# An attention and mixture-of-experts layer on one core: a hand-ordered opening, units loaded a head ahead, and a mixture stage in program order with norms and routing in pieces

## The chip, the core and the metric

The kernel runs on one core of one Trainium2 chip. The core has five engines that run their own instruction streams: TensorE (PE in the profile, with PEld for its weight loads), VectorE (DVE), ScalarE (ACT), GpSimd (POOL) and SyncE (SP), which here issues the DMAs. Matrix products go to PSUM, everything else lies in SBUF. The metric is device microseconds of one execution; lower is better.

## What is computed

One layer over 4 sequences of 512 tokens with 256 features. Each sequence has six vectors of modulation, made from a small condition `c`. The tokens are normalised and modulated, go through causal attention with 16 heads of 128, and are added back under a gate; then they are normalised and modulated again, go through a mixture of eight expert networks of different widths (plus one shared network and a "core" branch), and are added back under a second gate.

```python
mod = (silu(c) @ wmod).reshape(4, 6, 1, 256)
sa, ca, ga, sb, cb, gb = (mod[:, i] for i in range(6))
ga, gb = (sign(g) * maximum(abs(g), 0.25) for g in (ga, gb))
h = layernorm(x) * (1 + ca) + sa
# attention: 16 heads, causal
k, q, v = (einsum('ihd,bpd->biph', W, h) for W in (W_K, W_Q, W_V))
attn = softmax(masked(q @ k.T) / sqrt(128))
x = x + ga * einsum('df,bqf->bqd', W_O, flat(attn @ v))
h = layernorm(x) * (1 + cb) + sb
# mixture: each token's two best experts by softmax(h @ router_w + router_b - cost)
d = h @ down_w + down_b
out = sum over k in (0, 1) of gate_k * sum over e of (
    gelu(gelu(d * mask_ke) @ w1_e + b1_e) @ w2_e + b2_e)
out = out + 0.1 * (gelu(gelu(d) @ shared_w1 + shared_b1) @ shared_w2 + shared_b2)
x = x + gb * (out @ up_w + up_b + gelu(h) @ core_w + core_b)
```

## The kernel before

**Numbers in two parts.** Most products are made of three: a value `a` is kept as `hi` (its rounding to the type fp32r) and `lo` (the rest, `rest()`, line 148), and `mm3` multiplies lo by hi, hi by lo and hi by hi (lines 140 to 142). So nearly every matrix that PE reads first needs a cast, mostly on ScalarE, and a subtraction, on VectorE or GpSimd. Weights are loaded as "units" of 128 x 512 numbers into a `stage` tile (two buffers) and parted into `wu` tiles (`load_unit`, line 185).

**Opening.** `x0` (the first sequence) in two pieces, `c`, the matrix `wmod`, and the first units are loaded on SP's queue. sc = silu(c) is made by an Exp on ScalarE and three operations on VectorE. `normed` makes mean and variance (`bn_stats`, `bn_aggr`), rstd on GpSimd, and xn. `modulation` (line 301) makes the shift and scale of a norm from sc and wmod; `modulated` (line 378) transposes xn on PE, applies them and parts the result into hTh and hTl. `make_gates` (line 319) makes the gates ga and gb for all four sequences as rows of four partitions, with VectorE at lines 333 to 338, and stores them; `gate_rows` reads them back, spread over the partitions.

**Attention.** 64 heads in the order of `order`: four groups of four heads, in each group all four sequences b. For each head `n`: q and k (`project`), the values (`values`, tile pv, half of a pair of heads at a time), the scores of four tiles of 128 queries with maxima on VectorE (L488), Exp on ScalarE (L498), reciprocals (L502) and the scaling of `e` on GpSimd (L503, called `by_sum`). `turned` transposes e in blocks of 32 on VectorE, writes them out (`moved`) and reads them back as aT, so that blocks come to their places. `parted` casts aT on ScalarE (L535) and makes its rest on GpSimd (L148). `mixed` multiplies by the values (pz) and makes zh and zl; `project_out` multiplies by W_O (po), and after the last head of a group adds the gated result to x. `LAG = 3`: a head's aT is used three heads later. `finish` starts the second norm, its modulation and the routing of a sequence once its last head is done.

**Mixture.** `before_chunks` makes pd = h @ down_w, its Gelu on ScalarE and its two parts ghh and ghl on VectorE. `Mixture` goes through 20 chunks of 128 hidden features (`ORDER` has the experts) and the shared network: `first` makes ph, its Gelu (hid), and where it is needed the parts ah (ScalarE) and al (VectorE); `second`, three chunks later (`FFN_LAG`), multiplies by w2 into acc. `expert` turns acc into a part of the sum on VectorE (L859), which GpSimd adds to oacc (L863). `gelu_inputs` makes gelu(h) for the core branch on GpSimd and ScalarE; `core` multiplies it; `outputs` multiplies by up_w, applies the gate and stores y. `route` makes the two best experts and their gates with about thirty small operations on VectorE, over 32 partitions, with two or three Exp or Tanh on ScalarE, and stores them; each expert's row is read back as `spread`.

**Order.** PE's order is the program's (`manual_schedule`). The other engines' order in this version is set by a planner, which orders by a simulated time; only the first norm's VectorE and ScalarE work is in program order. `issue_after(i)` puts what follows behind instruction i in the planner's order. `later[n]` has work to be emitted beside head n.

Of the kernel before, what the change touches and what calls it, by code (L numbers as in the profile page):

```python
# [11 lines left out]
F32 = mybir.dt.float32  # L12
# [6 lines left out]
P = 128  # L19
# [4 lines left out]
HG = 4  # L24
# [71 lines left out]
FFN_CORE = (19, 20)  # L96
BEFORE3 = 4
EARLY = 2


TO_PART = tuple(u for u, (_, in_parts) in UNITS.items() if in_parts)
PART_AT = (18, 20, 22, 24, 26, 28, 34, 36, 38, 40, 42)
# [11 lines left out]
def adaln_attention_moe_kernel(  # L114
# [51 lines left out]

    load_x(0, 2)
    cT = const.tile([P, DC, B], F32, tag="cT", name="cT")
    nc.sync.dma_start(cT, c_t.rearrange("(c p) b -> p c b", p=P))
# [15 lines left out]
    def load_unit(src, nm: str, early: bool = False):  # L185

        st = work.tile([P, 512], F32, tag="stage", name=f"st_{nm}")
        nc.sync.dma_start(st, src)
        u = const.tile([P, 2, 512], F32R, tag="wu", name=nm, bufs=10)
        hi, lo = u[:, 0], u[:, 1]  # L190
        if early:
            nc.scalar.copy(hi, st)
        else:
            nc.gpsimd.tensor_scalar(hi, st, 1.0, 1.0, ALU.mult, ALU.mult)
        rest(nc.gpsimd, lo, st, hi)
        return hi, lo
# [62 lines left out]
    sc_e = small.tile([P, DC, B], F32, bufs=1, tag="silu_e", name="sc_e")  # L259
    exp_c = nc.scalar.activation(sc_e, cT, AF.Exp, scale=-1.0)  # L260
    nc.vector.tensor_scalar(sc_e, sc_e, 1.0, None, ALU.add)
    nc.vector.reciprocal(sc_e, sc_e)
    sc = small.tile([P, DC, B], F32, bufs=1, tag="silu", name="sc")
    nc.vector.tensor_mul(sc, cT, sc_e)

    ct = const.tile([P, C_END], F32, tag="cols", name="cols")
    nc.gpsimd.dma_start(ct, cols)
    b1 = ct[:, C_B1:C_B2]
    with tc.issue_after(exp_c.ins):
        nc.scalar.activation(gb1, b1[:, :NCH], AF.Gelu)  # L270
    load_wm(0)
    wqk_u[0] = load_unit(wqk[0], "wqk0", True)
    wv_u[0] = load_unit(wv[0], "wv0", True)
    load_wm(1)
    load_wm(2)
    wqk_u[1] = load_unit(wqk[1], "wqk1", True)
    for b in range(1, B):
        load_x(b)
# [3 lines left out]
    nc.vector.memset(router_w, 0.0)  # L282
    nc.sync.dma_start(router_w[:, :, :E], router.rearrange("p (c n) -> p c n", n=E))
# [8 lines left out]
    nc.vector.memset(mask[:, : NT - 1, :], 0.0)  # L292
    make_causal_mask(nc, mask[:, NT - 1, :], mask_val=MASKED)
    maskf = mask.rearrange("p t k -> p (t k)")
    def mod_w(c: int, f: int, n: int) -> bass.AP:
        return wm[f // 512, c][:, f % 512 : f % 512 + n]
# [4 lines left out]
    def modulation(which: int):  # L301
        pt = psum.tile([P, 4, B], F32, tag="pj", name=f"pt_mod_{which}", bufs=3)
        for i in range(4):
            for c in range(DC):
                nc.tensor.matmul(
                    pt[:, i, :],
                    lhsT=mod_w(c, 3 * D * which + i * P, P),
# [3 lines left out]
                )  # L311
        m = modT[:, 4 * which : 4 * which + 4, :]
        nc.vector.tensor_copy(m[:, :2, :], pt[:, :2, :])
        nc.vector.tensor_scalar(m[:, 2:, :], pt[:, 2:, :], 1.0, None, ALU.add)


    gates_d = dram.tile([B, 2, D], F32, tag="gates", name="gates_d")

    def make_gates():
        pm = psum.tile([B, 2, D], F32, tag="pj", name="pm", bufs=3)  # L320
        for i in range(2):
            for c in range(DC):
                nc.tensor.matmul(
                    pm[:, i, :],
                    lhsT=sc[:, c, :],
                    rhs=mod_w(c, (3 * i + 2) * D, D),
                    start=(c == 0),
                    stop=(c == DC - 1),
                )
        g = work.tile([B, 2, D], F32, tag="kh", name="g_raw")  # L330
        nc.scalar.copy(g, pm)
        sgn = work.tile([B, 2, D], F32, tag="kl", name="g_sgn")
        nc.vector.tensor_scalar(sgn, g, 0.0, 2.0, ALU.is_ge, ALU.mult)
        mag = work.tile([B, 2, D], F32, tag="tmp", name="g_mag")
        nc.vector.tensor_scalar(mag, g, -1.0, None, ALU.mult)
        nc.vector.scalar_tensor_tensor(mag, mag, 0.25, g, op0=ALU.max, op1=ALU.max)
        gates = work.tile([B, 2, D], F32, tag="tmp", name="gates")
        nc.vector.scalar_tensor_tensor(gates, sgn, 1.0, mag, op0=ALU.subtract, op1=ALU.mult)
        nc.sync.dma_start(gates_d, gates)
# [8 lines left out]
    def normed(b: int, which: int):  # L348
# [3 lines left out]
        for t in range(NT):  # L352
            nc.vector.bn_stats(st[:, t, :], xs[b][:, t, :])
        for t in range(NT):
            nc.vector.bn_aggr(mv[:, t, :], st[:, t, :])
# [3 lines left out]
        xn = work.tile([P, DC, NT, P], F32, tag="xn", name=f"xn_{b}_{which}", bufs=1)  # L359
# [9 lines left out]
        return xn  # L369
# [8 lines left out]
    def modulated(b: int, which: int):  # L378
# [6 lines left out]
        first = not (b or which)  # L385
        whole = []
        for c in range(DC):
            ptr = psum.tile([P, S], F32, tag="pj", name=f"ptn_{b}_{which}_{c}", bufs=3)
            for t in range(NT):
                nc.tensor.transpose(ptr[:, ts(t, P)], xn[:, c, t, :], ident)  # L390
            scale = modT[:, 4 * which + 2 + c, b : b + 1]
            shift = modT[:, 4 * which + c, b : b + 1]

            if c and not first:
# [3 lines left out]
            whole.append(ptr)  # L398

            for d in (c,) if not first else range(DC) if c == DC - 1 else ():  # L400
                nc.scalar.copy(hi[:, d, :], whole[d])
# [798 lines left out]
```

## Time and profile before

| what | value |
|---|---|
| median of three runs | 810.0 us (808.84 to 810.09) |
| the profiled execution | 809.29 us |
| its span, first to last instruction | 807.5 us |
| mean granted clock of TensorE | 0.986 |
| first matmul / first value product pv | 6.95 / 18.11 us from the span's start |
| stage of attention with heads of all kinds | to about 618 us |
| mixture | from there to the end |

The span is what the profile shows; about 1.8 us of the execution lie around it. Engine times are busy times, so an engine can be nearly always busy and still not be the reason that the kernel lasts: what counts is which engine the others wait for. PE's ends are modelled; the distance between starts of successive matmuls is the surer measure of its pace. The granted clock is TensorE's alone: where it is under 1, part of the stretch ran at half clock.

### The profile page before, as it was taken

What the parts mean: (1) busy time and instruction counts of PE and PEld (TensorE: products, weight loads), DVE (VectorE), ACT (ScalarE), POOL (GpSimd) and SP (SyncE); (2) the same over time, 40 slices, a digit from 0 to 9 for tenths busy, and PEclk for the clock granted to TensorE, in tenths of its full rate; (3) what the DMA queues carried; (4) which work ended last, traced back from release to release, by engine and by line L of the source; (5) the groups of instructions that cost most, each with busy time, mean ns of one, the idle gap of its engine ahead of it and who ended that gap; (6) DMA issues with size and microseconds to landing.
All of it is one profiled execution on the core that took longest, in us unless ns stands there. A gap on an engine that the chain in (4) does not pass through costs nothing. (4 is left out here: it accounts for less than half of the span.)

```text
span 807.5 us, 14122 instructions
## 1 busy us (share of the span) xinstructions
PE 775.5 (96%) x4487; PEld 671.9 (83%) x4487; DVE 594.7 (74%) x1734; ACT 490.9 (61%) x1184; POOL 521.7 (65%) x523
## 2 busy tenths in 40 slices
PE   6889999999999999999999999999997999989997
PEld 5669998999999999999999999998896866767775
DVE  5968788777777667676777677778898486785665
ACT  3556667666666655666666656666656333656663
POOL 4745566896767579786758886566546155655675
PEclk9999999999999999999999999999998899999999
DMA  7465354665666667675556765545575332312221
GB/s 236 112 190 152 111 156 128 184 180 160 199 192 182 182 204 220 174 213 177 177 175 186 191 178 151 162 137 160 147 227 156 106 124 86 105 53 77 55 86 58
DMA packets 73218, 124.12 MB, mean 154 GB/s; under 512 B 8996, under 2 KB 51252, under 8 KB 73144
## 3 DMA queue, kind: packets, MB, share of 16 engines
q1 hardware_dynamic: 73112, 123.21, 52.3%
q8 instruction: 36, 0.59, 0.3%
q14 instruction: 38, 0.31, 0.1%
q0 software_dynamic: 32, 0.02, 0.0%
HBM read 73.05 MB, written 50.14 MB: 153 GB/s over the span
## 5 line engine op out<-in xcount | busy, mean ns | idle before, releaser
L148 POOL TENSOR_TENSOR aT<-aT,aTh 128x1152 fp32r<-128x1152 f32 x64 | 172.0, 2687 | 115.5 <-ACT aTh L535 115.4
L503 POOL TENSOR_SCALAR e<-e,inv 128x128 f32<-128x128 f32 (+3 forms) x256 | 135.7, 543 | 69.3 <-DVE inv L502 67.2
L498 ACT ACTIVATE e<-e,nmax 128x128 f32<-128x128 f32 (+3 forms) x256 | 143.9, 564 | 45.4 <-DVE nmax L488 44.5
L535 ACT CAST aTh<-aT 128x1152 fp32r<-128x1152 f32 x64 | 74.2, 1159 | 134.8 <-DMA aT<-moved 81.3
L488 DVE CUSTOM_DVE_ANT_0 e<-ps,mask 128x128 f32<-128x128 f32 (+3 forms) x256 | 120.1, 478 | 23.8 <-PE ps L482 14.6
L518 DVE STREAM_TRANSPOSE T<-e 128x384 f32<-128x384 f32 (+2 forms) x256 | 100.3, 445 | 7.8 <-POOL e L503 7.8
L148 DVE TENSOR_TENSOR zl<-pz,zh 128x512 fp32r<-128x512 f32 x64 | 44.0, 688 | 52.8 <-ACT zh L553 52.7
L140 PE MATMUL ps<-kh,ql 128*128 128x256 f32 (+2 forms) x192 | 71.2, 371 | 6.3 <-DVE nmax L488 6.2
L140 PE MATMUL po<-wo,zl 128*128 128x256 f32 x256 | 73.1, 285 | 0.6 <-DVE zl L148 0.6
L141 PE MATMUL po<-wo,zh 128*128 128x256 f32 x256 | 72.0, 281 | 0.0
L142 PE MATMUL po<-wo,zh 128*128 128x256 f32 x256 | 72.0, 281 | 0.0
L140 PE MATMUL pv<-wv,hTl 128*128 128x256 f32 x256 | 71.8, 281 | 0.0
L141 PE MATMUL pv<-wv,hTh 128*128 128x256 f32 x256 | 71.6, 280 | 0.0
L142 PE MATMUL pv<-wv,hTh 128*128 128x256 f32 x256 | 71.5, 279 | 0.0
L863 POOL TENSOR_TENSOR oacc<-oacc,part 128x512 f32<-128x512 f32 x28 | 40.9, 1462 | 43.5 <-DVE part L859 36.8
L502 DVE RECIPROCAL inv<-tot 128x1 f32<-128x1 f32 x256 | 40.2, 158 | 37.2 <-ACT e L498 29.6
L141 PE MATMUL ps<-kl,qh 128*128 128x256 f32 (+2 forms) x192 | 65.5, 341 | 0.2
L140 PE MATMUL pz<-aTh,vl 128*128 128x512 f32 (+2 forms) x192 | 65.5, 341 | 0.0
L141 PE MATMUL pz<-aT,vh 128*128 128x512 f32 (+2 forms) x192 | 65.4, 341 | 0.0
L142 PE MATMUL pz<-aTh,vh 128*128 128x512 f32 (+2 forms) x192 | 65.4, 340 | 0.0
L142 PE MATMUL ps<-kh,qh 128*128 128x256 f32 (+2 forms) x192 | 65.0, 339 | 0.0
L592 POOL TENSOR_TENSOR x<-x,tmp 128x512 f32<-128x512 f32 x32 | 41.4, 1298 | 19.7 <-DVE tmp L590 19.5
(216 smaller groups left out, 2327.9 us busy)
## 6 DMA issues: line engine op xcount, KB each, us to landing
moved<-T SPq DMA_DIRECT2D x256, 160.0 KB, 2.8
aT<-moved SPq DMA_DIRECT2D x64, 640.0 KB, 3.9
spread<-gates_e SPq DMA_DIRECT2D x32, 256.0 KB, 3.3
st_wqk<-in_wqk SPq DMA_DIRECT2D x16, 256.0 KB, 3.8
wf_first<-wfp_first SPq DMA_DIRECT2D x5, 512.0 KB, 5.0
st_wv<-in_wv SPq DMA_DIRECT2D x8, 256.0 KB, 3.5
st_wo<-in_wo SPq DMA_DIRECT2D x8, 256.0 KB, 3.6
wmod<-in_wmod SPq DMA_DIRECT2D x6, 256.0 KB, 5.2
```

Of the source, the lines that this page charges most:

```text
L140: nc.tensor.matmul(o, lhsT=wl, rhs=mh, start=start, stop=False)
L141: nc.tensor.matmul(o, lhsT=wh, rhs=ml, start=False, stop=False)
L142: nc.tensor.matmul(o, lhsT=wh, rhs=mh, start=False, stop=stop)
L148: return eng.tensor_tensor(lo, full, f32(hi), ALU.subtract)
L488: least = nc.vector.tensor_tensor_reduce(out=et, in0=ps[:, :n], in1=maskf[:, S - n :], scale=-SCALE, scalar=BIG, op0=ALU.add, op1=ALU.min, ...
L498: exp = nc.scalar.activation(et, et, AF.Exp, bias=nm[:, t : t + 1], scale=-1.0, accum_out=tot[:, t : t + 1])
L502: nc.vector.reciprocal(inv[:, one], tot[:, one])
L503: by_sum = nc.gpsimd.tensor_scalar(et, et, inv[:, one], 1.0, ALU.mult, ALU.mult)
L518: nc.vector.transpose(to[:, first : first + n], blocks[:, at : at + (n - 1) * step + 1 : step])
L535: nc.scalar.copy(hi, full)
L592: nc.gpsimd.tensor_tensor(xu, xu, tmp, ALU.add)
L863: recent["added"] = nc.gpsimd.tensor_tensor(oacc, oacc, to, ALU.add).ins
```

## The change

In the opening, VectorE's, ScalarE's and PE's work up to the first q and k is written out in one function, `start`, in program order: statistics before sc, three of the four normalisations on VectorE and one on ScalarE, wqk0's rest on VectorE, hTh written by ScalarE from the transposes, and products with hTl after those with hTh. PE first multiplies 14 times by a tile of zeros, and three times between transposes and products. `c` and the columns `cols` are loaded on ScalarE's queue ahead of all else. The order of SP's first loads changes: the second sequence and the third unit now come before the rest of wmod.

The gates are made by columns (128 partitions) together with the second modulation beside head 1, transposed, and stored beside head 3; the router's parts move from the opening to head 8. Units are staged one head before they are parted, and their casts are ScalarE's. The cast of aT is placed after the head's last Exp and scaling.

`normed`, `modulated` and `route` become generators. For sequences 1 to 3 the second modulation and the routing (for 2 and 3 the norm too) are put in the list `beside`, and one piece of it is emitted beside each chunk (two per chunk from the seventh of the first sequence). From the end of attention on, VectorE, ScalarE and GpSimd are in program order. Gelu of h is made in parts at chunks 13, 17 and 19 (9, 11 and 13 for the last sequence), and the core branch's products move to chunks 4 and 5 of the next sequence.

```diff
-FFN_CORE = (19, 20)
+GELU_PARTS = (17, 19)
+FFN_CORE = (4, 5)
+WARM = 14
+FIRST_UNITS = (
+    ("wqk", 2, 0, 0), ("wqk", 3, 0, 1), ("wv", 1, 1, 0), ("wo", 0, 3, 0), ("wo", 1, 5, 0),
+)
-PART_AT = (18, 20, 22, 24, 26, 28, 34, 36, 38, 40, 42)
+PART_AT = (17, 19, 21, 23, 25, 27, 35, 37, 39, 41, 43)
...
+    nc.scalar.dma_start(ct, cols)
+    nc.scalar.dma_start(cT, c_t.rearrange("(c p) b -> p c b", p=P))
     load_x(0, 2)
...
     load_wm(0)
-    wqk_u[0] = load_unit(wqk[0], "wqk0", True)
-    wv_u[0] = load_unit(wv[0], "wv0", True)
-    load_wm(1)
-    load_wm(2)
-    wqk_u[1] = load_unit(wqk[1], "wqk1", True)
-    for b in range(1, B):
-        load_x(b)
+    st_qk = stage_unit(wqk[0], "wqk0")
+    st_v = stage_unit(wv[0], "wv0")
+    load_x(1)
+    st_qk1 = stage_unit(wqk[1], "wqk1")
+    with tc.issue_after(recent_dma[0]):
+        load_wm(1)
+        load_wm(2)
...
+    def keep_warm(n: int, tag: str):
+        pw = psum.tile([P, P], F32, tag=tag, name=f"pw_{tag}", bufs=1)
+        for _ in range(n):
+            nc.tensor.matmul(pw, lhsT=zeros, rhs=zeros, start=True, stop=True)
+    keep_warm(WARM, "av")
...
+    def second_modulation():
+        pt = psum.tile([P, 8, B], F32, tag="pj", name="pt_mod_1", bufs=3)
+        by_column(pt, 3 * D, 0)
+        by_column(pt, 2 * D, 4)
+        set_modulation(1, pt)
...
+        nc.vector.tensor_scalar(sgn3, raw, 0.0, 2.0, ALU.is_ge, ALU.mult)
+        nc.vector.tensor_scalar(mag3, raw, -1.0, 0.25, ALU.mult, ALU.max)
+        nc.vector.tensor_tensor(mag3, mag3, raw, ALU.max)
+        nc.vector.scalar_tensor_tensor(g, sgn, 1.0, mag, op0=ALU.subtract, op1=ALU.mult)
...
+    def start():
+        nc.scalar.activation(gb1, b1[:, :NCH], AF.Gelu)
+        nc.scalar.activation(sc_e, cT, AF.Exp, scale=-1.0)
...
+        wqk_u[0] = part_unit(st_qk, "wqk0", True, None)
...
+        norm(0)
+        norm(1)
...
+        last = norm(2)
+        nc.scalar.activation(xn[:, 3, :], x0[:, 3, :], AF.Identity, bias=shift, scale=rstd[:, 3:])
+        rest(nc.vector, wqk_u[0][1], st_qk, wqk_u[0][0])
+        set_modulation(0, pt)
+        with tc.issue_after(last.ins):
+            wv_u[0] = part_unit(st_v, "wv0", False)
...
+        keep_warm(3, "av")
+        for c in range(DC):
+            scale, shift = modT[:, 2 + c, 0:1], modT[:, c, 0:1]
+            nc.scalar.activation(hh[:, c, :], ptr[c], AF.Identity, bias=shift, scale=scale)
+            full = psum.tile([P, S], F32, tag="sc", name=f"full_0_0_{c}")
+            nc.vector.tensor_scalar(full, ptr[c], scale, shift, ALU.mult, ALU.add)
+            recent["norm"] = rest(nc.vector, hl[:, c, :], full, hh[:, c, :]).ins
+        wqk_u[1] = part_unit(st_qk1, "wqk1", True)
...
     def finish(n: int, b: int, h: int, z):
         project_out(b, h, z)
-        if h == H - 1:
+        if h < H - 1:
+            return
+        if b < 2:
             later.setdefault(n + 1, []).append((norm_batch, b, 1))
-            later.setdefault(n + 3 + (b > 1) + (BEFORE3 - 1) * (b > 2), []).append((modulate, b, 1))
-            later.setdefault(n + 4 + (b > 1) + (BEFORE3 - 1) * (b > 2), []).append((route, b))
+        if b == 0:
+            later.setdefault(n + 3, []).append((modulate, b, 1))
+            later.setdefault(n + 4, []).append((all_of, route, b))
+        else:
+            if b > 1:
+                beside.append(normed(b, 1))
+            beside.extend((modulated(b, 1), route(b)))
...
-    later[1] = [(make_gates,)]
+    later[1] = [(second_modulation,)]
+    later[3] = [(store_gates,)]
     for b in range(B):
-        later[2 + b] = [(gate_attention, b)]
-    later[2 + B] = [(modulation, 1)]
+        later[4 + b] = [(gate_attention, b)]
+    later[4 + B] = [(router_parts,)]
...
         if len(waiting) > 1:
-            part_one(-2)
+            with tc.issue_after(by_sum), tc.issue_after(exp):
+                part_one(-2)
...
+            for units, i, nm, st in staged_units:
+                units[i] = part_unit(st, nm, True)
+        staged_units.clear()
+        for nm, i in units_of(n + 1):
+            units, src = {"wqk": (wqk_u, wqk), "wv": (wv_u, wv), "wo": (wo_u, wo)}[nm]
+            staged_units.append((units, i, f"{nm}{i}", stage_unit(src[i], f"{nm}{i}")))
...
-                going.append((m, *begun))
+                going.append((m, *m.parts(*begun)))
+                for _ in range(2 if at >= 6 and not b else 1):
+                    next_piece()
                 at += 1
+                if before and k in FFN_CORE:
+                    before.core(len(before.pys))
...
+    ctx.enter_context(
+        tc.manual_schedule(
+            engines={mybir.EngineType.DVE, mybir.EngineType.Activation, mybir.EngineType.Pool}
+        )
+    )
     steps = all_ffn()
...
+        if n == N + 1:
+            with tc.issue_after(recent["z"]):
+                part_one(-1)
         if waiting:
             db, dh, aT = waiting.pop(0)
             done.append((db, dh, mixed(db, dh, aT)))
-        if n == N:
-            with tc.issue_after(recent["z"]):
-                part_one(-1)
```

## The prediction

> **What bounds the kernel now.** I read the page's busy row and slices first, then busy time by stretches, the waits of PE, and last the timeline where PE waits.
>
> ```profile
> PE 775.5 (96%) x4487; PEld 671.9 (83%) x4487; DVE 594.7 (74%) x1734; ACT 490.9 (61%) x1184; POOL 521.7 (65%) x523
> PEclk9999999999999999999999999999998899999999
> ```
>
> ```profile
> 0.00:18.11 18.11, 10.22 (x36) 8.24 (x37) 10.52 (x31) 6.58 (x11) 6.36 (x16) 1.00 0.81 263
> 18.11:80.00 61.89, 55.38 (x313) 47.34 (x312) 49.10 (x160) 36.90 (x96) 36.61 (x42) 0.94 0.53 145
> 80.00:580.00 500.00, 499.63 (x3155) 454.82 (x3155) 373.68 (x1198) 324.27 (x858) 349.94 (x359) 1.00 0.60 174
> 580.00:640.00 60.00, 54.54 (x305) 46.64 (x303) 48.84 (x163) 34.36 (x78) 32.16 (x30) 0.91 0.58 173
> 660.00:680.00 20.00, 17.04 (x72) 10.94 (x70) 17.86 (x36) 7.34 (x14) 14.69 (x14) 1.00 0.36 107
> 700.00:720.00 20.00, 16.91 (x61) 11.86 (x60) 19.82 (x38) 11.44 (x21) 15.62 (x11) 0.91 0.21 62
> ```
>
> Columns: stretch, length, busy of PE, PEld, DVE, ACT, POOL, granted clock, DMA. From 80 to 580 us PE is never idle (499.63 of 500): a faster VectorE, ScalarE or GpSimd buys nothing there. The loss is in four places: the start; 18 to 80; the seam to the mixture (580 to 640); two stretches of the mixture. I count each as PE idle plus (1 - clock) times the stretch: 6.5 + 3.7 = 10.2; 5.5 + 5.4 = 10.9; 3.0; 3.1 + 1.8 = 4.9. Together 29.0 us, besides the 18.11 us before the first value product pv and some 5 us after the last matmul.
>
> ```profile
> PE ps L140 <- DVE nmax L488: 6.2, 5, 1.9
> PE acc L140 <- ACT ah L816: 3.1, 1, 3.1
> PE ph L140 <- ACT hid L800: 2.7, 2, 2.1
> PE ph L141 <- DVE ghl L148: 1.9, 1, 1.9
> ```
>
> PE (line, then releaser: us in total, times, longest) waits for VectorE and ScalarE, never for data from outside. The timeline says what these were doing.
>
> ```profile
> 31.03 0.82 DVE L333 TENSOR_SCALAR g_sgn<-g_raw 4x512 f32<-4x512 f32 x1
> 31.78 1.50 DVE L335 TENSOR_SCALAR g_mag<-g_raw 4x512 f32<-4x512 f32 x1
> ...
> 44.66 1.16 ACT L535 CAST aTh<-aT 128x1152 fp32r<-128x1152 f32 x1 [2.02 <-DMA aT<-moved]
> ...
> 46.50 0.69 DVE L148 TENSOR_TENSOR kl<-pk,kh 128x512 fp32r<-128x512 f32 x1 [2.84 <-ACT kh L467]
> ...
> 660.10 0.27 DVE L638 TENSOR_TENSOR r_lg<-r_lg,r_m 32x128 f32<-32x128 f32 x1
> ...
> 704.25 1.06 DVE L638 TENSOR_TENSOR r_lg<-r_lg,r_m 32x128 f32<-32x128 f32 x1
> ```
>
> Gates on four partitions hold VectorE before PE's 1.50 us wait; a cast of aT stands at the head of ScalarE for 2.02 us until its transfer lands, kh behind it, and kl and the next maximum behind kh on VectorE, so that PE stood 1.49 us at 48.01; routing operations of 0.27 us take 1.06 when GpSimd runs beside them.
>
> [...] in the seam, 512-column products start 0.43 us apart (623.20, 623.63, 624.06), at full clock 0.23 (632.22, 632.46), so a stall costs more than itself. [...]
>
> **The change, part by part. The opening.** Columns and c leave the POOL and SP queues for ScalarE's: two issues of about 0.46 us (the price on SP), then a table load of 1.28 for Gelu, Gelu 0.22, a second load 1.28, Exp 0.21. Before, c was issued at 1.73 and landed about 6.0. Now at about 1.2: landing near 4 to 5.5, Exp near 6, sc near 6.3 to 7.2 instead of 6.9: about even. Ahead of it PE multiplies 14 times by zeros (two passes each, at most 0.22 us a pass, 6.2 us): nothing waits for them, they end about when sc is there, and PE is then at full clock, so pt_mod's 16 passes take 1.8 us instead of 3.57. Statistics no longer stand behind sc on VectorE (its second half waited from 5.2 to 6.36). The four normalisations took 3.33 us, 2.68 of that for two beside GpSimd's two unit remainders (1.26, 1.31); later, alone, four take 2.28. Now three run on VectorE, one on ScalarE, the remainder of wqk0 goes behind them (0.7 on VectorE) and wv0 goes to GpSimd afterwards: xn is done near 8.8, not 11.38; transposes 9.6; the modulation 9.7; ScalarE writes hTh straight from the transposes (0.6 each) at 10.4 and 11.0, where it was 13.39 and 14.25. PE starts q and k at 10.4 instead of 13.53. VectorE's two full (0.83) and two hTl (0.7) run from 9.75 to 12.8, so the last products with hTl end near 13.3, or 14.6 if sc is late. pv begins at 14.0 instead of 18.11: gain 4.1.
>
> On SP, wqk1's load now waits for a free buffer of two (near 9.5 to 10.5), and wm1, wm2, the next unit, rows, router and x2, x3 stand behind it. First needed of these is wqk1, by q of head 1 near 16: load 3.5 us, cast 0.62, remainder 1.3 end near 15.5. Cover is thin, 1 us at most is at risk. wm is needed a head later, x2 five.
>
> **Heads 0 to 7 (18 to 80 us).** Out go L333 to L338, 0.82 + 1.50 + 0.67 + 0.69 = 3.7 us of VectorE, for about six operations near 0.17 on 128 partitions; the wide modulation is on PE as before (32 passes against 16 and 8: 3.5 us both). Casts of aT now come after the head's last Exp, which ends the ScalarE waits that held q's and k's copies (2.02, 1.72, 2.95 us), and aT's remainder (2.68 on GpSimd) comes after e's scaling, behind which VectorE's transposes and next maximum stood before PE's wait of 1.91 at 60.11. Units' casts go from POOL (0.62) to ScalarE, loaded a head earlier. What is late next: VectorE itself. Before the first mixed head PE has only 6.0 us a head, while VectorE has ql, kl, vl 1.8, maxima 2.2, reciprocals 0.6, transposes 1.8 = 6.4, and the next batch's norm (1.4 + 0.6 + 2.3) and turning (2.2) in the first three heads. Against 22 us of PE there are about 27 of VectorE: 4.5 us stay. Gain 10.2 - 4.5 = 5.7. In the steady heads the aT cast has a head's slack (9.2 us) for 1.16 + 2.69, so nothing moves.
>
> **The seam.** Before, Gelu of pd, ghh and ghl stood behind routing of batch 1 (0.72, 1.02, 0.27) and statistics (0.73): PE waited 1.40 and 1.89, then ran 10 us at half clock. Batch 1's turning and routing now go into the mixture, in pieces. From the last score at 614.0: maximum to 614.75, Exp to 615.6, table 616.9, Gelu 617.6, ghh 618.3, ghl 619.0; PE's own work (pd, po, pz) lasts to 618.56. Stall about 0.3, and no half clock. Then the last head: transposed 621, moved and reloaded 8.3 us later (as before, 626.65 to 634.94), cast and remainder (1.16 + 2.66) to 633, where PE, two chunks and one head an iteration, wants it at 633.1. I leave 3.0 for that edge and for 582.5 (1.1), which stays. Gain 10.9 - 3.0 = 7.9.
>
> **The mixture.** Batch 1's routing came in one burst with GpSimd's gelu work, VectorE 19.82 of 20 us, and ah and al stood behind it. Now one piece goes beside a chunk (two in batch 0): batches 1 to 3 have 20, 29 and 29 pieces, and the routing of the last is ready at the end of batch 2. In batch 1 VectorE has al 13 x 0.68, sums 9 x 0.75, ghh, ghl, y 2.8, pieces about 12: 30 us in PE's 38, so order alone need not stall PE; three chunks (4.5 us) lie between ah and its use. Core moves behind the batch, with y, at no PE cost. The gate rows' load stays one per batch; GpSimd waits for it in order with its sums behind, which have some four chunks. I leave 3.0 of 7.9: gain 4.9.
>
> The end is untouched (oF, up, y): nothing.
>
> **Sum.** 4.1 + 5.7 + 7.9 + 4.9 = 22.6. The profiled execution took 809.29 (span 807.5, 1.8 around it): 786.7. The median shown is 810.0, 0.7 above: 787.4; with 0.6 for wqk1, 788.0.
>
> **Rivals.**
> *All stalls go:* 29.0 - 2 and 4.1: 810.0 - 31 = 779. For it: each stall has a named cause that the change touches. Against: VectorE's excess in the first heads.
> *Moved, not removed:* the opening's gain is kept (4.1), the seam's half (4), the rest returns as waits in order: 801. For it: PE was never short of work at the seam, so the last head's transfer can end late; fixed orders can't step round a wait. Against: slack of three chunks.
> *Slower:* in the mixture ScalarE's tanh, in order, waits for VectorE's piece[...], and the next chunk's Gelu stands behind both. Batches 0 to 2 have 63 chunks; above 0.36 us a chunk it eats the 22.6, and windows at half clock double it. At 0.5 us: 31.5, so 819 or more. For it: VectorE is full in both bad stretches. Against: only some 12 us of pieces a batch.
> *No change* has no mechanism of its own beyond these two meeting.
>
> **How the numbers follow.** Forecast 788 (782 to 795): 0.52. All gone 779: 0.14. Moved 801: 0.23. Slower 819: 0.09. No change 0.02 (within 0.2%, 1.6 us, about what this measurement can tell). Range 780 to 803 takes in the two faster rivals' centres nearly, leaving about 2 in 10. Unknown costs inside it: landing of c (-0.7 to +0.6), wqk1 (0 to 1), first heads (2 to 8 left), the seam's last head (0 to 4), pieces (0 to 8). Faster 0.89, same 0.02, slower 0.09.
>
> **What would show it.** First pv near 14; no aT cast before the head's last Exp; PE idle under 5 us from there to 75, no half clock; ghl within 0.5 us of PE's need at the seam; no VectorE stretch of 20 us above 19 after 640. Wrong if pv starts after 16.5, if PE waits for mixed(63)'s aT for 3 us, or if Gelu of hid waits behind tanh.

## The result, and the profile after

| | before | after |
|---|---|---|
| median (lowest to highest), four executions each | 810.05 us (808.84 to 811.35) | 800.49 us (799.75 to 802.16) |
| span of the profiled execution | 807.5 us | 800.4 us |
| mean granted clock in it | 0.986 | 0.991 |
| first pv | 18.11 us | 13.83 us |
| first ph (the mixture's first chunk on PE) | 620.23 us | 608.55 us |
| start of the last matmul | 802.13 us | 794.78 us |

The ratio is 0.9885, with a 95% interval of 0.9863 to 0.9906: 1.15% faster, 9.6 us where 22 were forecast. The profiled executions differ by 7.1 us; after's was the slowest of its four.

The page of the kernel after, its busy row and its row of granted clock:

```profile
PE 777.7 (97%) x4530; PEld 675.6 (84%) x4530; DVE 595.1 (74%) x1736; ACT 511.3 (64%) x1211; POOL 504.1 (63%) x495
PEclk9999999999999999999999999999999999999999
```

The eights of the row of before, at the seam, are gone. The same view by stretches as before, cut where the new stages lie (stretch, length, busy of PE, PEld, DVE, ACT, POOL, granted clock, DMA share, GB/s):

```profile
14.00:76.00 62.00, 61.23 (x379) 55.10 (x379) 52.18 (x180) 44.58 (x118) 34.69 (x42) 0.97 0.58 176
76.00:576.00 500.00, 497.03 (x3119) 453.37 (x3118) 375.15 (x1200) 340.41 (x872) 335.68 (x333) 1.00 0.60 174
576.00:633.00 57.00, 55.58 (x332) 47.55 (x331) 35.66 (x114) 33.71 (x71) 28.27 (x27) 1.00 0.58 180
653.00:673.00 20.00, 17.91 (x67) 11.52 (x66) 13.37 (x24) 10.34 (x18) 13.24 (x13) 0.91 0.22 81
693.00:713.00 20.00, 17.12 (x63) 11.62 (x62) 15.92 (x25) 11.58 (x19) 14.42 (x12) 0.91 0.16 53
```

The first heads and the seam are nearly full now: PE idles 0.8 of 62 us and 1.4 of 57. But the steady heads, full before (499.63 of 500), have lost 3 us, and two stretches of the mixture lose PE time and clock at once. The waits of PE (line, then releaser: us in total, times, longest) name the releasers:

```profile
PE ptn L448 <- DVE xn L418: 4.2, 4, 1.5
PE ps L151 <- DVE nmax L567: 3.0, 3, 2.2
PE acc L152 <- DVE al L159: 1.9, 2, 1.5
...
PE acc L151 <- DVE part L964: 1.2, 2, 0.7
PE ph L151 <- DVE ghh L848: 0.8, 1, 0.8
PE ph L151 <- ACT hid L900: 0.8, 1, 0.8
PE ph L152 <- DVE ghl L159: 0.2, 1, 0.2
```

The wait for ah (3.1) has gone, those for hid (2.7) and ghl (1.9) are down to 0.8 and 0.2. A wait for xn, 0.2 us in all before, is now the largest. The timeline shows it and the one in the steady heads (start, us, engine, line, operation):

```profile
537.52 4.03 DVE L418 TENSOR_SCALAR xn<-x,mv,rstd 128x256 f32<-128x256 f32 x4 [0.39 <-POOL rstd L413]
538.38 2.69 POOL L159 TENSOR_TENSOR aT<-aT,aTh 128x1152 fp32r<-128x1152 f32 x1
543.26 0.45 PE L151 MATMUL ps<-kh,ql 128*128 128x384 f32 x1 [2.25 <-DVE nmax L567]
...
650.50 2.64 POOL L975 TENSOR_TENSOR h2F<-hTh,hTl 128x512 f32<-128x512 f32 x2
651.61 4.30 DVE L418 TENSOR_SCALAR xn<-x,mv,rstd 128x256 f32<-128x256 f32 x4
653.11 2.66 POOL L968 TENSOR_TENSOR oacc<-oacc,part 128x512 f32<-128x512 f32 x2
654.63 0.33 PE L448 MATMUL ptn<-ident,xn 128*128 128x128 f32 x1 [0.70 <-DVE xn L418]
655.97 0.33 PE L448 MATMUL ptn<-ident,xn 128*128 128x128 f32 x1 [1.01 <-DVE xn L418]
...
706.14 0.33 PE L448 MATMUL ptn<-ident,xn 128*128 128x128 f32 x1 [1.54 <-DVE xn L418]
```

At 651.61 four normalisations take 4.30 us, with GpSimd's sums of h2F and oacc beside them: one takes 0.40, as it does alone, the other three 1.35 to 1.42 each. PE, in program order, already stands at their transposes. In the kernel before, the four of a second norm took 1.6 to 2.6 us, and in the mixture no transpose waited for them:

```profile
549.09 2.07 DVE L361 TENSOR_SCALAR xn<-x,mv,rstd 128x256 f32<-128x256 f32 x4
```

**Where the 7.1 us come from.** I took the starts of successive matmuls and counted, for each, how much later it came than its kind usually does (the median distance of the same operation and size in the same trace).

| stretch | before, us late | after, us late | gain | forecast |
|---|---|---|---|---|
| start of pv | | | 4.3 | 4.1 |
| first heads | 10.9 | 2.6 | 8.3 | 5.7 |
| steady heads, 520 to 580 | -0.3 | 4.9 | -5.2 | 0 |
| seam, 580 to 640 | 10.0 | 2.4 | 7.6 | 7.9 |
| mixture from 640 | 8.4 | 16.3 | -7.9 | 4.9 |

Opening, heads and seam together gained 20.2 where 17.7 were forecast. The forecast fell in the mixture, and in a stretch where nothing was to move.

The count leaves out 80 to 520, and that it adds up to 7.1 is in part chance. PE's order hardly differs between the two kernels, so the same matmul can also be set against itself. That gives 4.3 at the first scores, 8.8 more up to 82 us of before, 0.6 lost from there to 546, 4.1 lost by 566, 7.9 gained by 639, and 8.9 lost from there to the last matmul (7.35 in all). The lines of the table are good to about 1 us.

### The profile page after: what moved, and what is told of

It reads as the page before. It is cut to its first block, busy times and chain, and to the rows that moved or that the text cites. A ratio compares the mean times of both kernels' runs of the same rounds, so it can differ in the third digit from the quotient of the medians.

```text
span 800.4 us, 14197 instructions
## 1 busy us (share of the span) xinstructions
PE 777.7 (97%) x4530; PEld 675.6 (84%) x4530; DVE 595.1 (74%) x1736; ACT 511.3 (64%) x1211; POOL 504.1 (63%) x495
## 5 line engine op out<-in xcount | busy, mean ns | idle before, releaser
L159 POOL TENSOR_TENSOR aT<-aT,aTh 128x1152 fp32r<-128x1152 f32 x64 | 171.2, 2675 | 16.7 <-ACT aTh L614 9.2
L567 DVE CUSTOM_DVE_ANT_0 e<-ps,mask 128x128 f32<-128x128 f32 (+3 forms) x256 | 122.9, 486 | 56.8 <-PE ps L153 40.5
L632 ACT CAST zh<-pz 128x512 fp32r<-128x512 f32 x64 | 37.6, 588 | 78.6 <-PE pz L628 78.4
```

The costliest lines, as they stand in the source:

```text
L159: return eng.tensor_tensor(lo, full, f32(hi), ALU.subtract)
L567: least = nc.vector.tensor_tensor_reduce(out=et, in0=ps[:, :n], in1=maskf[:, S - n :], scale=-SCALE, scalar=BIG, op0=ALU.add, op1=ALU.min, ...
L632: recent["z"] = nc.scalar.copy(zh.rearrange(by_block, a=NB, r=R), pz).ins
```

## The experiments

All were timed beside the kernel before (its medians 809.9 to 811.1). Each is an edit of the kernel after, unless it says otherwise. Theory P, placing: the fixed order puts xn one piece ahead of its transposes and beside GpSimd's sums; PE meets them late. Theory D: VectorE is slowed beside GpSimd and late as a whole. Other rivals: the gain of the mixture's new arrangement was never there; the fixed order costs as such; VectorE is simply full.

| run | median us | ratio to before, interval |
|---|---|---|
| e1_turn_later | 794.60 | 0.9817 [0.9793, 0.9840] |
| e2_planner | 795.17 | 0.9821 [0.9803, 0.9839] |
| e3_opening_only | 801.00 | 0.9892 [0.9874, 0.9910] |
| e4_gelu_early | 798.98 | 0.9861 [0.9840, 0.9883] |
| e5_planner_later | 795.49 | 0.9820 [0.9803, 0.9838] |
| e6_norm_split | 795.00 | 0.9818 [0.9805, 0.9830] |
| e7_cast_free | 817.26 | 1.0090 [1.0069, 1.0112] |
| e8_no_warm | 803.93 | 0.9930 [0.9912, 0.9948] |
| e9_split_behind | 794.87 | 0.9803 [0.9782, 0.9824] |
| e10_gate_rows | 804.51 | 0.9921 [0.9900, 0.9942] |
| e11_xn_act | 794.54 | 0.9798 [0.9774, 0.9821] |
| e12_all | 795.62 | 0.9808 [0.9786, 0.9830] |
| e13_no_prep | 789.17 | 0.9736 [0.9708, 0.9763] |
| e14_no_top | 788.14 | 0.9733 [0.9706, 0.9760] |
| e15_neither | 785.94 | 0.9708 [0.9679, 0.9737] |
| e16_prep_dve | 792.21 | 0.9764 [0.9738, 0.9790] |
| e17_prep_dve_xn | 793.90 | 0.9786 [0.9760, 0.9811] |

### What is the placing of the transposes worth?

e1 starts the normalisations two pieces earlier and leaves the transposes where they are, so that three pieces and not one lie between the last normalisation and the first transpose:

```diff
-        for _ in range(5):
+        for _ in range(3):
             yield
...
+        for _ in range(2):
+            yield
```

> The turning of a norm comes two chunks later after its last normalisation (two of the five empty pieces before the normalisations are moved behind them; the number of pieces stays). Theory P (TensorE reaches the transposes before VectorE has made xn, and stands in order): the 4.2 us of waits for xn go, with two windows at half clock (1.7 us each): 793 to 795. Theory D [...]: TensorE waits for al and the sums instead, 799 to 801.

5.9 us faster than after. Waits of PE of e1:

```profile
PE ps L151 <- DVE nmax L569: 2.6, 2, 2.2
PE acc L152 <- DVE al L159: 1.9, 2, 1.5
PE acc L151 <- DVE part L966: 1.4, 3, 0.7
...
PE ptn L450 <- DVE xn L418: 0.6, 1, 0.6
```

The wait for xn falls from 4.2 to 0.6, and the two half-clock windows (3.4 us each at a granted clock of 0.51, at 657.1 and 708.3 in after) do not occur (1.00 in every stretch of e1 from 633 on). From the first ph to the last matmul the mixture takes 180.1 us, against 186.2 in after. Placing is shown as the cause of these 6.

e2 takes the fixed order of VectorE, ScalarE and GpSimd away from the mixture:

```diff
-    ctx.enter_context(
-        tc.manual_schedule(
-            engines={
-                mybir.EngineType.DVE,
-                mybir.EngineType.Activation,
-                mybir.EngineType.Pool,
-            }
-        )
-    )
```

> The mixture keeps its pieces, but VectorE, ScalarE and GpSimd are ordered by the planner again. Theory O (the fixed order is what costs in the mixture, 16.7 us above back-to-back matmuls from 640 on): at most 796. If the pieces alone or their place cost it: 800 to 802. If the fixed order is what makes the pieces work: 804 or more.

795.17: with the planner's order the waits for xn are gone too. Both edits together (e5):

> Both at once: the turning two chunks later, and VectorE, ScalarE and GpSimd ordered by the planner in the mixture. If the later turning (794.6 alone) and the planner (795.2 alone) remove the same waits: 793 to 796. If they remove different ones: 789 to 791.

795.49, no better than either, as was expected if they remove the same loss: with the transposes placed well, the fixed order costs nothing that this measurement can tell.

e11 leaves the transposes where they were and takes xn of sequences 2 and 3 off VectorE:

```diff
+                nc.scalar.activation(
+                    xn[:, :, t, :],
+                    xs[b][:, t, :].rearrange("p (c d) -> p c d", c=DC),
+                    AF.Identity, bias=back[:, t : t + 1], scale=rstd[:, t : t + 1],
+                )
```

> The change with the normalisations of sequences 2 and 3 on ScalarE (activation with scale and bias) in place of VectorE; nothing else moves. Theory P (TensorE stands because xn is late in VectorE's order): waits for xn go though the turning stays one chunk behind, 793 to 796. Theory D (VectorE as a whole is short beside GpSimd): al and the sums come earlier too, 790 to 793. If ScalarE's order makes new waits: 798 or more.

794.54: a third way to the same loss. e4 moves GpSimd's sums away from xn instead:

```diff
-                if k == (9 if at_end else 13):
+                if k == 9:
...
-                if k + 6 * at_end in GELU_PARTS:
+                if k + 6 in GELU_PARTS:
```

> Gelu of h and its parts on GpSimd at chunks 9, 11 and 13 of every sequence (as for the last one), so not beside the normalisations of the next but one. Theory D [...]: waits for xn under 1 us, 794 to 797. Theory P: xn waits shrink by what xn shortens, about 2 us in all: 798 to 800.

Only 1.5 us, and the interval overlaps that of after. The wait for xn falls to 1.3, but GpSimd's sums now meet the last routing pieces of the sequence, and PE waits 4.0 us at another place (timeline of e4):

```profile
688.10 2.99 POOL L975 TENSOR_TENSOR h2F<-hTh,hTl 128x512 f32<-128x512 f32 x2
688.61 1.25 DVE L756 TENSOR_SCALAR r_g<-r_g 32x16 f32<-32x16 f32 x1
697.57 0.47 PE L151 MATMUL acc<-ah,wf_second 128*128 128x512 f32 x1 [3.96 <-DVE mv L410]
```

An operation on 16 numbers per partition takes 1.25 us there, beside GpSimd's sums (1.5 us each). This is the first sign of a second cause.

### What is all of the mixture's and seam's new arrangement worth?

e3 keeps the opening and attention of after and sets the mixture as before: routing and second norms beside the heads, Gelu of h in one burst, no fixed order:

```diff
-FFN_CORE = (4, 5)
+FFN_CORE = (19, 20)
...
-            beside.extend((modulated(b, 1), route(b)))
+            later.setdefault(n + 3 + (b > 1) + (BEFORE3 - 1) * (b > 2), []).append((modulate, b, 1))
+            later.setdefault(n + 4 + (b > 1) + (BEFORE3 - 1) * (b > 2), []).append((all_of, route, b))
...
-                    m.gelu_parts(GELU_PARTS.index(k + 6 * at_end))
+                if k == 10:
+                    with tc.issue_after(recent["added"]):
+                        m.gelu_inputs()
+                        for c in range(DC):
+                            m.gelu_parts(c)
```

> The opening and the attention part of the change alone; mixture, second norms, routing, core and gelu of h as before the change. My count by stretches (start 4.6, heads 7.6 gained, seam 8 gained and mixture 8 lost in the change) gives 798 to 801: the mixture's part is worth nothing. If the prediction's step holds (mixture and seam gain 12.8): 811 or more. If the mixture's part loses as a whole: under 797.

801.0 against 800.5: on balance the new arrangement gave nothing. The old waits come back as the seam's loss (waits of PE of e3):

```profile
PE ph L152 <- DVE ghl L159: 3.3, 1, 3.3
PE acc L151 <- ACT ah L916: 3.1, 1, 3.1
...
PE ph L151 <- ACT hid L895: 2.1, 1, 2.1
```

So the 7.6 us of the seam are real, and the mixture gave them back.

### What holds the other half?

With xn's stall gone the mixture is no better than before: by the count of starts 10.0 us late from 640 on in e1, 8.4 in before, where 3.0 were forecast. What PE waits for is small and scattered: al, part, hid. The timeline of e1 at the largest of these:

```profile
740.47 1.30 POOL L159 TENSOR_TENSOR gxl<-h2F,gxh 128x512 fp32r<-128x512 f32 x1
740.64 1.27 DVE L760 TENSOR_TENSOR lt<-lt,r_g 32x128 f32<-32x128 f32 x1
741.84 0.27 DVE L761 TENSOR_TENSOR lt<-lt,r_g 32x128 f32<-32x128 f32 x1
742.04 0.73 DVE L966 SCALAR_TENSOR_TENSOR part<-acc,idle,spread 128x512 f32<-128x512 f32 x1
743.34 1.33 DVE L159 TENSOR_TENSOR al<-hid,ah 128x512 fp32r<-128x512 f32 x1
744.72 0.50 PE L152 MATMUL acc<-al,wf_second 128*128 128x512 f32 x1 [1.53 <-DVE al L159]
```

L760 and L761 have one size; the one beside GpSimd's rest takes 1.27 us, the other 0.27. al stands behind both, and takes 1.33 itself beside GpSimd's next operations (0.69 alone). Two causes are possible: GpSimd's work, or the pieces' place ahead of al. e13, e14 and e15, all on e1, take away the one, the other, and both.

e13 (GpSimd's preparation of gelu(h) left out, and with it the low part of the core branch):

```diff
-            nc.scalar.activation(hF, hF, AF.Gelu)
-            nc.gpsimd.tensor_scalar(gxh[:, c, :], hF, 1.0, 1.0, ALU.mult, ALU.mult)
-            rest(nc.gpsimd, gxl[:, c, :], hF, gxh[:, c, :])
+            nc.scalar.activation(self.gx[0][:, c, :], f32(hh[:, c, :]), AF.Gelu)
```

> The kernel with the turning one chunk later, with GpSimd's work for gelu(h) left out in all four sequences (h2F is not summed, gelu is taken of hTh alone and written by ScalarE, and the core branch multiplies this one part twice, so the core branch's low part is left out). It takes 2 x 1.35, 2 x 0.65 and 2 x 1.30 us of GpSimd out of each sequence, and nothing of VectorE's or PE's. Theory contention: what the mixture still loses with the turning moved (10.0 us of starts later than back to back after 640 us, 794.6 in all) is VectorE working beside GpSimd, so that al is late; then 789 to 792, and the waits for al and part (3.3 us) fall below 1.5. Theory order: al stands behind routing pieces in VectorE's order, whatever GpSimd does: 793.5 to 795.

e14 (routing of sequences 2 and 3 left out; they use the gates of sequence 1):

```diff
         nc.vector.transpose(lt, pl)
+        if b > 1:
+            routed[b] = routed[1]
+            return
```

> The kernel with the turning one chunk later, with the routing of sequences 2 and 3 left out after its products and the turning of its logits: about 27 small VectorE operations, three Tanh and one store each; these sequences use the gates of sequence 1. PE's work is the same. Theory order: al comes behind routing pieces, and the mixture's rest of 10.0 us falls by 3 to 6: 789 to 792. Theory contention: the pieces are only the victims, and GpSimd's sums beside al and part stay: 793 to 795.

> Both left out, GpSimd's work for gelu(h) in all sequences and the routing of sequences 2 and 3. If either one alone takes the mixture's rest away, this is no faster than the better of the two; if they are two losses side by side, it is the sum of both gains. If neither matters, 794 to 795, and the rest is a matter of PE's own order (new batches waiting for ghh and hid).

| | median us | first ph to last matmul, us |
|---|---|---|
| after | 800.49 | 186.2 |
| e1 | 794.60 | 180.1 |
| e13, no preparation on GpSimd | 789.17 | 173.2 |
| e14, no routing of 2 and 3 | 788.14 | 173.5 |
| e15, neither | 785.94 | 171.2 |

Each theory alone predicted one of the first two to stay near 794; both fell, by 5.4 and 6.5 us, and together by 8.7, not 11.9. So both count, and taking either away takes most of the loss with it. That the two do not add is near the noise of the medians; the stage lengths show it more clearly (6.9 and 6.6 us less, 8.9 together). In e13 the same operation is short again and PE's wait for al is gone (timeline, then waits of PE, of e13):

```profile
737.87 0.28 DVE L760 TENSOR_TENSOR lt<-lt,r_g 32x128 f32<-32x128 f32 x1
```

```profile
PE acc L152 <- DVE al L159: 0.3, 1, 0.3
```

The traces say how each counts. From the first ph to the last matmul VectorE's same 234 operations take 140.9 us, their durations added, in e1 and 128.5 in e13: al 41.2 and 33.7, xn 8.9 and 5.5, routing 34.6 and 32.9. So GpSimd's preparation lengthens al itself far more than the routing pieces; these make al late mainly by standing ahead of it. Two rivals can be set aside. VectorE is not simply full: e15 gains its time in the chunks of sequences 2 and 3 (3.9 and 3.1 us less than in e1), and there VectorE is busy 34.0 of 40.4 and 28.8 of 45.8 us in e1. And GpSimd's own lateness is not it: VectorE waits for GpSimd's oacc for 4.7 us in e1, 3.7 in e13 and 6.7 in e14.

e16 takes GpSimd's preparation away without leaving work out: VectorE and ScalarE prepare gelu(h), GpSimd does not (on e1):

```diff
-                nc.gpsimd.tensor_tensor(
+            nc.vector.tensor_tensor(
...
-            nc.gpsimd.tensor_scalar(gxh[:, c, :], hF, 1.0, 1.0, ALU.mult, ALU.mult)
-            rest(nc.gpsimd, gxl[:, c, :], hF, gxh[:, c, :])
+            nc.scalar.copy(gxh[:, c, :], hF)
+            rest(nc.vector, gxl[:, c, :], hF, gxh[:, c, :])
```

> The kernel with the turning one chunk later, nothing left out, but the preparation of gelu(h) taken from GpSimd: VectorE makes the two sums (0.68 us each, at chunks 13 and 15, for the last sequence 9 and 11) and the two rests (0.68), ScalarE the two casts (0.62). If the mixture's rest is the meeting of GpSimd's long operations with routing pieces on VectorE, VectorE is better off by doing 2.7 us more itself: 789 to 792, waits for al and part below 1.5 us. If VectorE is simply full between chunks 13 and 19, its added 2.7 us a sequence make it worse: 795 to 799.

792.21, at the edge of what was expected, and 176.5 us from the first ph to the last matmul: with 2.7 us more a sequence given to VectorE the stage is 3.6 us shorter. Waits for al and part are 1.6 us (under 1.5 was expected). It is the fastest complete kernel of this study, 2.4% under before by its ratio; against e1 the two intervals hardly part (0.9790 and 0.9793). e17 makes the same change to e11, with xn on ScalarE and the transposes where after has them:

> The same preparation on VectorE and ScalarE, with the normalisations of sequences 2 and 3 on ScalarE (0.6 us each) instead of the turning one chunk later. If VectorE's load is what remains, the 4.6 us less of VectorE make this 1 to 3 us faster than the run before it; if only meetings with GpSimd mattered, the two are within 1 us.

793.90 (178.4 us). Against e11 (794.54, and 179.0 us) that is a gain within the noise, so the worth of moving the preparation is shown on one base only. Nor is e17 faster than e16, though it has less work on VectorE: no sign that VectorE's mere load is what remains.

### The wait in the steady heads

e6 and e9 (both on e1) draw the norm of sequences 0 and 1 over two heads, e9 also behind each head's last operations:

```diff
-            later.setdefault(n + 1, []).append((norm_batch, b, 1))
+            later.setdefault(n + 1, []).append((some, 8))
+            later.setdefault(n + 2, []).append((some, 9))
```

> The later turning, and the second norm of sequences 0 and 1 in two parts beside two heads, so that two normalisations at a time and not four (4.03 us beside GpSimd's rest of aT) stand before a maximum on VectorE. If this order is behind TensorE's wait of 2.2 us near 540, present in the change and in all four kernels so far: the wait falls under 0.6, 791.5 to 793. If VectorE is simply behind there: 794 to 796.

> The later turning, and the second norm of sequences 0 and 1 in two parts, each put behind the second maximum, Exp and scaling of its own head (in the run before, the planner drew both parts together again and nothing changed). If four normalisations in a row on VectorE are the cause of TensorE's 2.2 us near 540: that wait under 0.6, 791.5 to 793. If not: 794 to 796.

Neither did anything, since neither parted the four normalisations (timeline of e6):

```profile
538.88 4.03 DVE L418 TENSOR_SCALAR xn<-x,mv,rstd 128x256 f32<-128x256 f32 x4 [0.39 <-POOL rstd L413]
544.62 0.44 PE L151 MATMUL ps<-kh,ql 128*128 128x384 f32 x1 [2.25 <-DVE nmax L569]
```

So these edits did not do what they were for, and say nothing of the cause. e12, with e9 and e11 in one, gave 795.62 and keeps the wait too:

> Later turning, norm in two parts behind their heads, and normalisations of sequences 2 and 3 on ScalarE together. If each removes its own waits: 789 to 791. If the later turning and ScalarE's normalisations remove the same: 791.5 to 794.

The cause, by the traces, is GpSimd's rest of aT, which now comes after the scaling of e. Of the four normalisations of after three take 0.40 to 0.70 us; the one that meets the rest (2.69 us, from 538.38) takes 2.75. e7, below, in which the planner places the cast and so the rest, shows the other case: no rest runs beside the four, they take half the time, and PE waits for no maximum between 525 and 575 us (timeline of e7):

```profile
553.37 2.10 DVE L418 TENSOR_SCALAR xn<-x,mv,rstd 128x256 f32<-128x256 f32 x4
```

e7 moves much else as well; a run that changes this meeting alone was not made.

### What the opening's and heads' parts are worth

e7 lets the planner place the cast of aT again:

```diff
-            with tc.issue_after(by_sum), tc.issue_after(exp):
-                part_one(-2)
+            part_one(-2)
```

> The change with the planner free to place the cast of aT (nothing puts it behind the head's last Exp and scaling). The prediction's reason for the first heads: the waits of ScalarE at casts of aT come back, TensorE stands twice for 1.5 to 2 us and at half clock between 18 and 80: 804 to 807. Rival (the gates alone held VectorE): 799 to 802.

817.26, far above what was expected: in the changed kernel the cast's place is worth 17 us. Setting the same scores of e7 and after against each other, 8 us are lost by 67 us of after and 6 more by 152. All waits of e7, then its timeline at one of them:

```profile
POOL aT L159 <- ACT aTh L614: 132.6, 48, 5.9
...
ACT aTh L614 <- DMA aT<-moved: 62.1, 25, 5.5
```

```profile
57.94 1.15 ACT L614 CAST aTh<-aT 128x1152 fp32r<-128x1152 f32 x1 [5.53 <-DMA aT<-moved]
59.16 0.59 ACT L546 CAST kh<-pk 128x512 fp32r<-128x512 f32 x1
59.78 0.69 DVE L159 TENSOR_TENSOR kl<-pk,kh 128x512 fp32r<-128x512 f32 x1 [3.15 <-ACT kh L546]
```

The cast stands at the head of ScalarE for 5.53 us with kh behind it, and kl behind kh. PE waits 3.47 us for a maximum at 65.91, and a half-clock window follows at 67.1 (512-column products start 0.42 us apart there, 0.23 before). In after, ScalarE waits 3.9 us for that transfer in the whole run, where it waited 81.3 in before. Why e7, with 62.1, is slower than even the kernel before stays open.

e8 leaves out the products with zeros:

```diff
-    keep_warm(WARM, "av")
...
-        keep_warm(3, "av")
```

> The change without the products of zeros. The prediction's price: 16 passes of the first modulation at half clock cost 1.8 us, and q and k start cold (0.2 us for each of 12): first pv 2 to 4 us later, 802.5 to 804.5. Rival (the chain of norm and sc sets the start, the clock is warm in time anyway): 800 to 801.

803.93, and pv starts at 17.40. Its opening on PE:

```profile
6.90 3.73 PE L349 MATMUL pt_mod<-sc,wmod 128*128 128x4 f32 x16 [6.90 <-DMA wmod<-in_wmod]
10.49 1.95 PE L1134 MATMUL ptn<-ident,xn 128*128 128x128 f32 x8
```

In after, 14 of the 16 take 1.73 us, and the eight transposes 1.07. Then come the first of q and k: 0.43 us from one 512-column product to the next in e8 (13.68 and 14.11), 0.23 in after (10.57 to 12.42). So about 3.6 of the 4.3 us by which pv comes earlier depend on the products with zeros, by PE's pace behind them, where the forecast gave that pace 1.8 of 4.1. The view by stretches gives 1.00 as the granted clock of both openings; only the pace shows the difference. (The other runs with the opening of after start pv at 13.40 to 14.72, so the share is not sharp.)

e10 makes the gates as rows of four partitions again, at head 1, with the operations of before:

```diff
-    later[1] = [(second_modulation,)]
-    later[3] = [(store_gates,)]
+    later[1] = [(make_gates,), (second_modulation,)]
```

> The change with the gates as rows of four partitions again (3.7 us of VectorE beside head 1, as before the change). The prediction's price: TensorE stands 2.7 us more between 25 and 40 and loses a window of half clock (1.7): 804 to 806. Rival (with the casts in their place, head 1 has room for it): 800 to 802.

804.51: by the medians the columns are worth 4.0 us, by the ratios 2.9, and the two intervals just overlap (0.9900 and 0.9906). The number came as expected, but not its reason. Beside head 1, where the rows hold VectorE from 27.13 to 30.72, PE waits 0.15 us. The loss is 30 us later (timeline of e10, then of after):

```profile
55.64 4.29 DVE L417 TENSOR_SCALAR xn<-x,mv,rstd 128x256 f32<-128x256 f32 x4
61.65 0.44 PE L151 MATMUL ps<-kh,ql 128*128 128x384 f32 x1 [2.05 <-DVE nmax L566]
```

```profile
55.88 1.94 DVE L418 TENSOR_SCALAR xn<-x,mv,rstd 128x256 f32<-128x256 f32 x4
```

In e10 the rest of aT starts at 56.77, beside the normalisations; in after it starts at 59.65, behind them. It is the meeting of the steady heads again, in another place. What the gates' form itself is worth beside head 1 is not shown; the columns even have a price there, a half-clock window at 25.7 that e10 lacks (last section).

## Why the prediction was wrong

- **Opening: right**, 4.3 for 4.1, but in part by luck. The split differs: without the products of zeros pv comes only 0.7 us earlier than before (e8), where the forecast gave 2.3 to the new order. Its price of four normalisations "alone", 2.28, was read at 28.8, where GpSimd ran beside them; alone they take 0.40 each. Its 16 passes of the first modulation at 1.8 us came nearly so (3.57 in before; in after 14 of them take 1.73), and so did its two table loads of 1.28 (before has them at 0.73 and 6.26, after at 1.73 and 3.73).
- **Heads 0 to 7: better**, 8.3 for 5.7. One named cause was right, the cast (e7); for the other, the gates, e10 gives the time but not the reason. The term that was mis-sized is VectorE's excess of 4.5 us, which did not appear: between 14 and 36 VectorE is busy 17.93 us, where 27 were put against 22 of PE, and PE idles 0.8 us between 14 and 76. "No half clock" is wrong by one window, at 25.7: the forecast priced the wide modulation in time (3.5 us, measured 3.66), not in clock.
- **"In the steady heads ... nothing moves": wrong**, 5.2 us lost in the profiled execution (4.1, near 543, when the same matmuls are compared). The step looked at the cast's slack and not at whom GpSimd's moved rest would run beside; it now runs beside the four normalisations near 537, PE waits 2.25 us, and in this execution a half-clock window follows (0.51 from 544.5 to 547.9).
- **The seam: right**, 7.6 for 7.9, by a sum whose parts shifted. ghl is 0.23 us late (0.5 was allowed), and the last head's edge, for which most of 3.0 was kept, has no wait; the first chunk waits 1.0 in all for ghh and ghl, where 0.3 was put.
- **The mixture: this is the step that failed.** "I leave 3.0 of 7.9: gain 4.9", and 7.9 were lost. It rests on "30 us in PE's 38, so order alone need not stall PE", which fails twice. First the place: in a fixed order a sum that fits is not enough. PE's transposes were one piece behind xn, with none of the slack of "three chunks" that ah has; that cost 6 us (e1, e2, e11). Then the sizes: the sum has al at 0.68 and the pieces at 12, and in after, in the chunks of sequence 1, 14 al take 13.1 us, the pieces 16.9, and VectorE is busy 37.5 of 43.0 us. Operations were priced at their lone durations, though the forecast itself shows L638 at 0.27 and 1.06, and two normalisations of the opening at 2.68 beside GpSimd; it lists the pieces among its unknowns as 0 to 8. With the place mended, leaving out GpSimd's preparation gives 5.4 us more (e13), two routings 6.5 (e14). With both taken away 1.2 us late from 640 on remain (e15); that a complete kernel can come down to the 3.0 is not shown.
- **The rivals.** "Moved, not removed" gave the time (801; its terms, 4.1 and 4, give 802), and its reason, that fixed orders can't step round a wait, holds: PE stands 4.2 us at xn in after, 0.2 in before. The rest is luck: the seam gained all of its 7.6 and not half, and the wait was at the second norms and not at the seam's last head. The lengthening that "Slower" rests on is there too (L638 takes up to 1.40 us in before, L760 1.27 in e1 beside GpSimd's rest, each near 0.27 otherwise), but too small to make the kernel slower than before; tanh ahead of Gelu costs 0.8 us, once.

Beside GpSimd xn grew as routing did: in after a normalisation takes 0.40 us alone, 1.35 to 1.42 beside GpSimd's sums (1.32 each), and 2.75 beside the rest of aT (2.69), so about as long as the operation that it meets. The forecast counted on this for routing alone.

## What to carry to other kernels

When an order is fixed by hand, ask of every wait how far its producer stands ahead in the consumer's order, in time, with durations as they are beside the neighbours they will have: a sum of work that fits says nothing of it. Price small operations at their contended duration (here 1.27 us for 0.27, and 2.75 for 0.40) where a long GpSimd operation is placed near, and place the two apart; giving the long one to the engine that it disturbs is worth a trial (it gained in e16, and nothing clear in e17). When a variant's time comes out as expected, look where in the trace it arose: in e10 it was not where the theory said. A cast that waits for a transfer (5.53 us in e7, with kh and kl behind it) belongs behind all that its engine owes to the critical path.

## What was not expected of the hardware

Half clock came here behind PE work that has no gap. In after, the second modulation and the gates are 32 products of four columns each, one behind the other:

```profile
22.21 3.66 PE L350 MATMUL pt_mod<-sc,wmod 128*128 128x4 f32 x32
```

A window of half clock of 3.41 us begins at 25.7 (granted clock 0.50 until 29.1), and no wait of PE lies between 21 and 31. All 17 runs with these 32 products in a row have such a window, begun between 24.7 and 29.9 us, during the products or within 1.3 us of their end. e10, with 16 of them (1.95 us, at 24.30), has none there (1.00 from 14 to 76), and neither has before, whose 16 take 1.85 us at 79.19 (1.00 from 79 to 90). Why is not shown.

Short waits of PE are followed by a half-clock window in some executions and not in others. One of 2.25 us, up to 543.26 in after, was, and two of 0.70 and 1.01, up to 654.63 and 655.97, were (0.51 in both windows); before has a window at 61.3 (0.51), after a wait of 1.91 up to 60.11. But after the same wait of 2.24 or 2.25 us in e1, e9 and e12, PE keeps its pace (512-column products 0.23 us apart) to the end of the view near 550, where those of after start 0.43 apart from 544.64. What decides it is not shown. Executions of one kernel differ in their clock: e1's go from 793.67 us at 0.997 to 797.19 at 0.993.
